# Moving store and load issues between the queues of a two-layer attention and spectral-convolution kernel: stores from SyncE to ScalarE two steps later, branch-matrix loads from SyncE to GpSimd

## The chip, the cores and the metric

The kernel runs on one core of one Trainium2 chip. A core has five engines with instruction streams of their own: TensorE (PE in the profile; its weight loads are shown apart as PEld), VectorE (DVE), ScalarE (ACT), GpSimd (POOL) and SyncE (SP). Any of ACT, SP and POOL can issue a DMA here; the profile shows the issuing part of an engine with a trailing q (SPq, ACTq, POOLq). The metric is the device time in microseconds (us) of one execution, and the median over the runs is compared.

## The reference

The input `x` has the shape (2, 128, 64, 64): two images, 128 channels, 64 x 64 positions. There are two layers.

```python
# layer 0, on x transposed to (2, 64, 64, 128)
x = LN(neighbourhood_attention_7x7(LN(x)) ) @ w1.T + x      # 4 heads of 32
x = LN(relu(LN(x) @ w2.T)) @ w3.T + x
# layer 1, on the tokens t of each image, (2, 4096, 128)
q   = LN(t)
sim = q @ q.T / sqrt(128);  sim[diagonal] = -1e9
t   = t + softmax(sim) @ q
u   = LN(t)
t   = t + sum over the 4 branches of  w[branch] * stu(u[: fraction], branch)
# stu: 16 causal filters phi of the sequence's length, by FFT,
#      once on u and once on u with alternating signs,
#      each filter's output through M_phi_plus[branch, k] or M_phi_minus[branch, k],
#      scaled by sigma[k] ** 0.25, summed over k; plus a three-tap filter M_u[branch]
```

The four branches use the whole sequence, a half, a quarter and an eighth of it, and their weights come from a hard Gumbel softmax over four numbers. The kernel combines the four branches' matrices with these weights first (per segment of the sequence), and so applies one set of matrices.

## The kernel before

**Stages.** By time in the profiled execution: layer 0 until about 345 us; the self-attention of image 0 from about 345 to 830 us; that of image 1 from 830 to 1242 us; leftover pieces of the work filled in until about 1300 us, called the end in what follows; and the spectral convolution from 1300 us on, which is a long row of small PE products (`burst` and `project`, L1565 and L1584) with copies out of PSUM by DVE and ACT. The convolution in the frequency domain reads its input from two arrays in DRAM: `us`, the transformed tokens, and `gs`, the transformed filters.

**The attention, `attention(b, fill)`.** The 4096 tokens of an image are 8 chunks of 512. As the similarity matrix is symmetric, only the 36 pairs (a, c) of chunks with a <= c are computed. Each pair takes four steps. For a pair, PE makes the similarities in a PSUM bank (`bank`, L927 or L936), ACT takes their exponential into `e` (L932 or L943), one pair ahead of its use. PE then multiplies `e` with the tokens for the rows of chunk c (`other`, L1057). The same weights are needed transposed for the rows of chunk a (`own`, L985). Pairs with a = c need no transposed half: there PE uses `es[j]` at once (L949 transposes the part under the diagonal, and the diagonal's products are also recorded at L985). For all "far" pairs (a != c, and not the last neighbours 6 and 7) the transposition goes over DRAM:

- `sent` (L959): ACT issues the write `eb<-e`, 1 MB, after the pair's fourth exp. There are four `eb` buffers in DRAM and two `e` buffers.
- `moved` (L966), two steps (MOVE) later: SP issues four reads `et<-eb` of 256 KB that put the blocks of 32 rows in their transposed place. There are two `et` buffers.
- `turned` (L975), seven steps (TURN) after the write: DVE transposes within blocks of 32 x 32.
- `pair_onto`/`onto` (L985), from eight steps (DELAY) after the write on: PE's `own` products.

Within the attention, from some 430 us on, the program order of PE, DVE, ACT, POOL and SP is the order in which the Python code issues the instructions (a manual schedule); before that, only the marked instructions keep it. So an instruction that waits holds all later ones of its engine.

**The work filled in, `fill()`.** At each step the attention calls `fill()`. It first calls `stores()`, which issues all DMA writes that the earlier steps appended to the list `behind_`, and then advances one generator by one step:

```python
        def stores():
            while behind_:
                to, src = behind_.pop(0)
                nc.sync.dma_start(out=to, in_=src)
```

The generators that matter here:

- `after(b, c)` finishes chunk c of image b, 16 chunks in all. It divides by the softmax's sum (L1105 transposes `xa` in a bank), adds the residual, normalises to `z` (the line L174 `ln_rs`, on POOL, is its power), and then makes a forward transform in three groups of products (`tr` and `z`, L1156 and L1169). For each group, ACT copies the banks to `uo` (L1138, two buffers), the `adder` (POOL) makes sums and differences `ub` (L1141, four buffers), and DMA writes `us<-ub` are appended (L1145 and L1148): 4, 4 and 8 of them for the three groups, so 16 for a chunk and 256 in all.
- `branch_weights` loads four matrices `m_u` (`st<-in_m_u`), combined on DVE with the branches' weights `wt`.
- `filters` loads the filters (`pn`) on SP, transforms them (L1360) and makes `fb` and `fn` on POOL (L1372, L1383; they share the four `ub` buffers); 32 DMA writes `gs<-fb` and `gs<-fn` are appended (L1347).
- `for_ffn` calls `filter_matrices`, which loads 32 blocks of `m_plus` and `m_minus` (`st`, two buffers in each of two pools), three ahead of their use, and combines them on DVE to `mpl` and `mmi` (L1299 and L1301). Then SP loads `inv` (L1499) and the first blocks `ct` and `ut` of the convolution (L1459 and L1467).
- `short_lags` makes the three-tap filter: it writes `xa` back by transposes and ACT copies, and multiplies with `mu` (lag products).

All branch loads (`m_u`, `m_plus`, `m_minus`) go through `branch()` (L1274 to L1278):

```python
            st = (pool or sp).tile([P, 4, P], F32, tag="st", name="st")[:, 0 : src.shape[1]]
            nc.sync.dma_start(out=st, in_=src[i].rearrange("k d e -> d k e"))
```

**The end.** After the second attention `adder` becomes DVE, and the generators that are left, two chunks and their `short_lags`, are advanced in turn with a `stores()` after each step. Then come the residual's lag products (`residuals`) and the convolution, whose input is read on SP (`ct` and `ut`) as long as it runs.

Of the kernel before, what the change touches and what calls it, by code (L numbers as in the profile page):

```python
# [14 lines left out]
P = 128  # L15
# [87 lines left out]
def kernel(  # L103
# [16 lines left out]
    nc = tc.nc  # L120
# [14 lines left out]
    for c in range(4):  # L135
# [23 lines left out]
        out=flip, in_=flip, compare_op=ALU.not_equal, fill=1.0, base=1 - QT * QT, pattern=[[0, 2], [1, QT * QT]],  # L159
# [16 lines left out]
    def ln_statistics(src):  # L176

        n = src.shape[1]
        st = lnp.tile([P, 4, 6], F32, tag="ln_st", name="ln_st")
        mv = lnp.tile([P, 4, 2], F32, tag="ln_mv", name="ln_mv")  # L180
        rs = lnp.tile([P, 4], F32, tag="ln_rs", name="ln_rs")
        for j in range(n):
            nc.vector.bn_stats(st[:, j, :], src[:, j, :])
            nc.vector.bn_aggr(mv[:, j, :], st[:, j, :])
        rsqrt(rs[:, :n], mv[:, :n, 1], 1e-5)
        return mv, rs

    def ln_apply(dst, src, stats):
        mv, rs = stats
        for j in range(src.shape[1]):  # L190
            nc.vector.tensor_scalar(
                dst[:, j, :], src[:, j, :], mv[:, j, 0:1], rs[:, j : j + 1], ALU.subtract, ALU.mult
            )
# [5 lines left out]
    def transposed(ps, src):  # L199

        for j in range(src.shape[1]):
            nc.tensor.transpose(ps[:, j * P : (j + 1) * P], src[:, j, :], ident)  # L202
# [37 lines left out]
    with l0a:  # L240
# [34 lines left out]
        def table(ci, h, eng):  # L275
# [16 lines left out]
            out=gavg, in_=gavg, compare_op=ALU.is_ge, fill=0.0, base=0,  # L292
# [3 lines left out]
            out=gavg, in_=gavg, compare_op=ALU.is_ge, fill=0.0, base=3,  # L296
# [11 lines left out]
        for h in range(HEADS):  # L308
            src = bass.AP(rpb.tensor, rpb.offset + h * RPR * RPW + 50, [[RPW, QT], [1, QT], [1, RLEN]])
# [567 lines left out]
    with ap_:  # L877
# [6 lines left out]
        def bank():  # L884
            return ps_m.tile([P, 512], F32, tag="bank", name="bank")
# [5 lines left out]
            out=tr.rearrange("p h e c -> p (h e) c"),  # L891
            in_=nc.inline_tensor(t_in, "t_in").ap().rearrange("(h p) c -> p h c", p=P),
# [195 lines left out]
        adder = [nc.gpsimd]  # L1088
        behind_ = []

        def stores():
            while behind_:
                to, src = behind_.pop(0)
                nc.sync.dma_start(out=to, in_=src)


        def after(b, c):

            yield True
            n0 = 4 * c  # L1100
            par, hf = divmod(c, 4)
            hh, fp = divmod(hf, NFP)
            pt = bank()
            for j in range(4):
                nc.tensor.transpose(pt[:, j * P : (j + 1) * P], xa[b][:, (n0 + j) * P : (n0 + j + 1) * P], ident)  # L1105
            rden = sp.tile([P, 4], F32, tag="rden", name="rden")
            kept_, out_ = tt[b][:, n0 : n0 + 4, :], pt.rearrange("p (j d) -> p j d", d=P)
            nc.vector.reciprocal(rden, out_[:, :, P - 1])
            rest = sp.tile([P, 4], F32, tag="rest", name="rest")
            nc.vector.tensor_reduce(rest, out_[:, :, 0 : P - 1], AX.X, ALU.add)  # L1110
            for j in range(4):
                nc.vector.scalar_tensor_tensor(
                    kept_[:, j, 0 : P - 1], out_[:, j, 0 : P - 1], rden[:, j : j + 1], kept_[:, j, 0 : P - 1],
                    ALU.mult, ALU.add,
                )
            nc.vector.tensor_tensor(rest, rest, rden, ALU.mult)
            nc.vector.tensor_tensor(kept_[:, :, P - 1], kept_[:, :, P - 1], rest, ALU.subtract)
            yield
            borrowed = b == 1 and spare not in ([], [None])
            z = spare.pop() if borrowed else sp.tile([P, 4, P], F32, tag="z4", name="z4")  # L1120
            stats = ln_statistics(kept_)
            yield True
            yield True
            ln_apply(z, kept_, stats)
            yield
            yield True
            pt = bank()
            transposed(pt, z)
            s0 = 1 + 2 * P * hh * FB
            to = zc[b][:, par, s0 : s0 + 2 * P * FB].rearrange("p (c e f) -> p e f c", e=2, f=FB)  # L1130
            nc.scalar.copy(to[:, :, 2 * fp : 2 * fp + 2], pt.rearrange("p (e f c) -> p e f c", e=2, f=2))
            yield

            def store(pu, n, r0, m, ri):

                for s in range(2):
                    both = sp.tile([P, 512], F32, tag="uo", name="uo", bufs=2)
                    nc.scalar.copy(both[:, 0 : 2 * n], pu[s][:, 0 : 2 * n])  # L1138
                    ub = sp.tile([P, 2, 256], F32, tag="ub", name="ub", bufs=4)
                    for sgn, op in enumerate((ALU.add, ALU.subtract)):  # L1140
                        adder[0].tensor_tensor(ub[:, sgn, 0:n], both[:, 0:n], both[:, n : 2 * n], op)  # L1141
                    for sgn in range(2):
                        to = us[r0 : r0 + m, sgn, :, 2 * hh + s, 2 * fp : 2 * fp + 2, b, par, :]
                        if ri is not None:
                            behind_.append((to[:, ri], ub[:, sgn, :].rearrange("p (f d) -> p f d", d=P)))  # L1145
                            continue
                        for f in range(2):
                            behind_.append((to[:, :, f].rearrange("k i d -> i k d"), ub[64 * f : 64 * f + 64, sgn, 0:P]))  # L1148

            for r0, c0 in row_tiles:  # L1150
                for ri in range(2):
                    pu = [bank() for _ in range(2)]
                    for e in range(2):
                        for s in range(2):
                            rows_ = slice(s * 64, (s + 1) * 64)
                            nc.tensor.matmul(  # L1156
                                pu[s][:, e * 256 : (e + 1) * 256], lhsT=tr[rows_, hh, e, c0 + ri * P : c0 + (ri + 1) * P],
                                rhs=z[rows_, 2 * e : 2 * e + 2, :].rearrange("p f d -> p (f d)"), start=True, stop=True,
                            )
                    store(pu, 256, r0, P, ri)  # L1160
                    if FB == 4 or ri:
                        yield

            pu = [bank() for _ in range(2)]
            for e in range(2):
                for f in range(2):
                    for s in range(2):
                        rows_ = slice(s * 64, (s + 1) * 64)
                        nc.tensor.matmul(  # L1169
                            pu[s][f * 64 : (f + 1) * 64, e * P : (e + 1) * P], lhsT=tr[rows_, hh, e, left_col:],  # L1170
                            rhs=z[rows_, 2 * e + f, :], start=True, stop=True,
                        )
            store(pu, P, left_row, 32, None)
            yield

            if borrowed:
                spare.append(None)
# [96 lines left out]
        def branch(src, i, pool=None):  # L1274

            st = (pool or sp).tile([P, 4, P], F32, tag="st", name="st")[:, 0 : src.shape[1]]
            nc.sync.dma_start(out=st, in_=src[i].rearrange("k d e -> d k e"))
            return st.rearrange("p k e -> p (k e)")  # L1278

        def filter_matrices(mpl, mmi, pool):  # L1280
# [36 lines left out]
        def filters():  # L1317
# [24 lines left out]
            def store(src, r0, n, ri, s, i, o):  # L1342
                to = bass.AP(
                    gs.tensor, gs.offset + r0 * 4 * SG * GROW + (i * SG + s) * GROW + o * LL,
                    [[4 * SG * GROW, n], [2 * SG * GROW, 2], [1, LL]],
                )
                behind_.append((to, src))  # L1347

            everything = [(r0, c0 + ri * P, (ri,), P) for r0, c0 in row_tiles for ri in range(2)]
            everything.append((left_row, left_col, (0, 1), 64))  # L1350
            for r0, c0, parts_, m in everything:
                places = cm[1][:, SG * LL : (3 * SG) * LL].rearrange("p (j e c) -> p j e c", j=SG, e=2)
                for j in range(SG):
# [21 lines left out]
                    for at, ri in enumerate(parts_):  # L1375
                        mine = slice(at * n, (at + 1) * n)
                        store(fb[mine], r0, n, ri, s, 0, ri)
                        if ri == 0:
                            store(fb[mine], r0, n, ri, s, 1, 1)
# [136 lines left out]
        while chains:  # L1516
            for gen in chains[:2]:
                if next(gen, 0) == 0:
                    chains.remove(gen)
                stores()  # L1520
            next(kept[0], None)
        for _ in residuals:
            next(kept[0], None)
        for _ in kept[0]:
# [11 lines left out]
    with ExitStack() as cv:  # L1536
# [133 lines left out]
        def place_of(o, par, a):  # L1670
            return o[:, :, a % 2, a // 2, :, par].rearrange("p c f -> p f c")
# [68 lines left out]
        for h in range(2):  # L1740
# [12 lines left out]
            for par in range(2):  # L1753
                for a in range(4):
                    to = place_of(o, par, a)
# [100 lines left out]
```

## Time and profile before

| | |
|---|---|
| median of 3 runs | 2059.06 us (2057.91 to 2060.68) |
| the profiled execution | 2061.56 us, its span 2059.8 us |
| mean granted clock of TensorE | 0.971 |
| SP's hardware queue (q1) | 162.59 MB, 32.1% of the time of 16 DMA engines |
| ACT's hardware queue (q10) | 58.04 MB, 7.0% |
| POOL's software queue (q0) | 576 packets, 2.10 MB, 0.3% |
| writes `eb<-e`, on ACT | 54 of 1024 KB |
| reads `et<-eb`, on SP | 216 of 256 KB |

The span is the time from the first to the last instruction of the profiled execution; the metric has some 1.8 us around it. A row of the profile names a line of the kernel, the engine, and the operation as out<-in with shapes. A wait is written as waiter <- releaser, and its time is idle time of the waiting engine just before an instruction. In the waits of a queue (SPq) the wait of the issuing engine before a DMA goes out is meant. Idle time of an engine that is not the bottleneck costs nothing by itself.

### The profile page before, as it was taken

The numbers are of one execution on the slowest core, as the hardware profiler recorded it, in microseconds if no ns is written. First come the engines' busy times: TensorE is split into PE (matmuls) and PEld (weight loads), VectorE is DVE, ScalarE is ACT, GpSimd is POOL, SyncE is SP. The second block draws the span as 40 slices with busy tenths as digits, with TensorE's granted clock in tenths as the row PEclk, the third lists the DMA queues.
The fourth block names the chain that finished last, engine by engine and source line by source line (L and its number), as shares of the span: only waits on it lengthen the run. The fifth ranks groups of instructions, "written<-read, shape, count | busy, mean of one in ns | idle before, by whom it ended". The sixth has DMA issues, their size and how long they took to land.

```text
span 2059.8 us, 50961 instructions
## 1 busy us (share of the span) xinstructions
PE 1924.6 (93%) x20504; PEld 1355.8 (66%) x20504; DVE 941.0 (46%) x2918; ACT 733.1 (36%) x1718; POOL 570.6 (28%) x954
## 2 busy tenths in 40 slices
PE   6899998999899999897978898999999999999998
PEld 4677775444444444443433344799999899999987
DVE  5799995443544343242533336333333334333332
ACT  3789885312223323222312232222222222222222
POOL 4467986303422113101101111022222121222211
PEclk8999999999999999999989999999999999999999
DMA  5222221667656534648865632222222123222211
GB/s 153 62 62 62 62 58 31 191 149 232 188 154 178 159 108 150 172 119 209 226 173 160 182 112 73 70 68 67 66 67 60 51 56 103 68 66 67 67 45 43
DMA packets 278378, 225.97 MB, mean 110 GB/s; under 512 B 122607, under 2 KB 241535, under 8 KB 270720
## 3 DMA queue, kind: packets, MB, share of 16 engines
q1 hardware_dynamic: 269442, 162.59, 32.1%
q10 hardware_dynamic: 8126, 58.04, 7.0%
q8 instruction: 163, 2.67, 0.5%
q0 software_dynamic: 576, 2.10, 0.3%
q14 instruction: 71, 0.58, 0.1%
HBM read 131.40 MB, written 91.25 MB: 108 GB/s over the span
## 4 chain that ended last, share of the span: by engine, by line
PE 75%; DVE 8%; DMA 5%; POOL 4%; issue 4%; ACT 1%; SPq 1%; DVEq 0%; POOLq 0%; ACTq 0%
PE acc L1584 27%; PE own L985 10%; PE bank L927 7%; PE pc L1565 7%; PE other L1057 6%; PE bank L349 2%; PE bank L559 2%; PE bank L202 2%; PE bank L1156 2%; DMA et<-eb 2%; PE bank L1199 1%; DMA eb<-e 1%; DVE et L975 1%; PE bank L523 1%; PE po L581 1%
## 5 line engine op out<-in xcount | busy, mean ns | idle before, releaser
L1570 DVE COPY y<-pc 128x512 f32<-128x512 f32 x320 | 206.1, 686 | 347.4 <-PE pc L1565 345.9
L1584 PE MATMUL acc<-y,mpl 32*128 32x256 f32 x5120 | 324.9, 380 | 0.8 <-DVE af L1594 0.8
L1584 PE MATMUL acc<-y,mmi 32*128 32x256 f32 x5120 | 316.5, 375 | 0.0
L1570 ACT COPY y<-pc 128x512 f32<-128x512 f32 x320 | 171.9, 589 | 392.7 <-PE pc L1565 379.1
L1584 PEld LDWEIGHTS acc<-y,mpl 32*128 32x128 f32 x5120 | 289.9, 186 | 8.3 <-DVE af L1594 1.3
L1584 PEld LDWEIGHTS acc<-y,mmi 32*128 32x128 f32 x5120 | 290.9, 185 | 3.9
L985 PE MATMUL own<-et,tok 128*128 128x512 f32 x448 | 225.9, 629 | 61.2 <-DVE et L975 49.1
L932 ACT ACTIVATE e<-bank 128x512 f32<-128x512 f32 x216 | 128.8, 599 | 308.0 <-PE bank L927 302.7
L1057 PE MATMUL other<-e,tok 128*128 128x512 f32 x448 | 230.9, 597 | 6.5 <-DVE xa L1066 6.5
L927 PE MATMUL bank<-cm 128*128 128x512 f32 x432 | 227.3, 608 | 0.0
L1565 PE MATMUL pc<-ct,ut 32*128 32x256 f32 x2560 | 212.5, 377 | 3.1 <-DVE y L1570 3.1
L1595 POOL TENSOR_TENSOR af<-af 128x512 f32<-128x512 f32 x39 | 49.7, 1275 | 589.2 <-DVE af L1594 589.2
L985 PEld LDWEIGHTS own<-et,tok 128*128 128x128 f32 x448 | 86.9, 199 | 177.5 <-issue 108.7
L1565 PEld LDWEIGHTS pc<-ct,ut 32*128 32x128 f32 x2560 | 172.7, 186 | 9.3 <-DVE y L1570 5.2
L975 DVE STREAM_TRANSPOSE et<-et 128x1024 f32<-128x1024 f32 x108 | 127.7, 1221 | 67.6 <-DMA et<-eb 66.3
L174 POOL TENSOR_TENSOR ln_rs<-ln_rs,mhalf 128x4 f32<-128x4 f32 x24 | 25.3, 1054 | 480.6 <-DVE ln_rs L173 480.5
L1057 PEld LDWEIGHTS other<-e,tok 128*128 128x128 f32 x448 | 81.6, 191 | 100.0 <-issue 84.0
L1141 POOL TENSOR_TENSOR ub<-uo 128x256 f32<-128x256 f32 (+1 forms) x160 | 96.5, 640 | 178.1 <-ACT uo L1138 167.5
L927 PEld LDWEIGHTS bank<-cm 128*128 128x128 f32 x432 | 76.9, 194 | 73.5 <-issue 67.8
L546 ACT ACTIVATE p<-p,mn 128x196 f32<-128x196 f32 x256 | 114.4, 449 | 14.4 <-DVE mn L536 13.8
L1138 ACT COPY uo<-bank 128x512 f32<-128x512 f32 (+1 forms) x96 | 46.9, 517 | 125.3 <-PE bank L1156 96.6
L943 ACT ACTIVATE e<-bank 128x512 f32<-128x512 f32 (+1 forms) x72 | 32.6, 455 | 139.0 <-DVE bank L941 133.9
(261 smaller groups left out, 2559.7 us busy)
## 6 DMA issues: line engine op xcount, KB each, us to landing
eb<-e ACTq DMA_DIRECT2D x54, 1024.0 KB
et<-eb SPq DMA_DIRECT2D x216, 256.0 KB
ut<-us SPq DMA_DIRECT2D x160, 128.0 KB
us<-ub SPq DMA_DIRECT2D x128, 128.0 KB
ct<-gs SPq DMA_DIRECT2D x320, 40.0 KB
vw<-vd SPq DMA_DIRECT2D x256, 49.0 KB
ct<-gs SPq DMA_DIRECT2D x320, 32.0 KB
vd<-v SPq DMA_DIRECT2D x128, 32.0 KB
```

The source lines that it names most:

```text
L546: nc.scalar.activation(p, p, AF.Exp, bias=t[name + "mn"][:, h : h + 1], scale=-1.0, accum_out=t["den"][:, u, h : h + 1],)
L927: nc.tensor.matmul(ps.rearrange("p (q t j) -> p q t j", q=4, t=4), lhsT=cm[b][:, n * P : (n + 1) * P], rhs=keys.rearrange("p (t q j) -> p ...
L932: nc.scalar.activation(e, ps.rearrange("p (q r) -> p q r", q=4), AF.Exp, bias=0.0, scale=ASCALE)
L975: in_place(nc.vector.transpose(flat, flat))
L985: nc.tensor.matmul(out_, lhsT=tok[b][:, n, :], rhs=e, start=first, stop=last, skip_group_check=True)
L1057: nc.tensor.matmul(turn(other, "p (q r) -> p q r"), lhsT=tok[b][:, n, :], rhs=es[j], start=(j == 0), stop=(j == 3),)
L1138: nc.scalar.copy(both[:, 0 : 2 * n], pu[s][:, 0 : 2 * n])
L1141: adder[0].tensor_tensor(ub[:, sgn, 0:n], both[:, 0:n], both[:, n : 2 * n], op)
L1565: nc.tensor.matmul(pcs[j].rearrange("p (g o c) -> p o g c", g=4, o=2)[:, :, at], lhsT=ut[rows_, par, :], rhs=cv_[rows_], start=True, stop= ...
L1570: (nc.scalar.copy if j % 2 else nc.vector.tensor_copy)(y[:, :, :, 4 * kl + j, :], pcs[j].rearrange("p (g x k) -> p k g x", g=4, k=KF))
L1584: nc.tensor.matmul(acc[j][:, 0:256], lhsT=(mmi if l else mpl)[rows_, k, :], rhs=y[rows_, k, 2 * l : 2 * l + 2].rearrange("p s n x -> p (s ...
L1595: eng.tensor_tensor(af[:, 0:2], af[:, 0:2], af[:, 2:4], ALU.add)
```

## The change

Three things change. `stores()` issues its DMA writes on ACT. It takes a second list: the sums append to `fresh_`, and what is in `fresh_` moves to `behind_` at the end of a call, so that a write goes out at the second call of `stores()` after its sums were issued. `branch()` issues its loads on POOL. As the last writes would now be left in the two lists, two more calls of `stores()` stand after the leftover generators. SP keeps the reads `et<-eb`, the loads of `pn` and `inv`, and the blocks `ct` and `ut`.

```diff
@@ attention and fill @@
         behind_ = []
 
+        fresh_ = []
+
         def stores():
-            while behind_:
-                to, src = behind_.pop(0)
-                nc.sync.dma_start(out=to, in_=src)
+            for to, src in behind_:
+                nc.scalar.dma_start(out=to, in_=src)
+            behind_[:] = fresh_
+            fresh_.clear()
@@ store() in after(): the us writes @@
                         if ri is not None:
-                            behind_.append((to[:, ri], ub[:, sgn, :].rearrange("p (f d) -> p f d", d=P)))
+                            fresh_.append((to[:, ri], ub[:, sgn, :].rearrange("p (f d) -> p f d", d=P)))
                             continue
                         for f in range(2):
-                            behind_.append((to[:, :, f].rearrange("k i d -> i k d"), ub[64 * f : 64 * f + 64, sgn, 0:P]))
+                            fresh_.append((to[:, :, f].rearrange("k i d -> i k d"), ub[64 * f : 64 * f + 64, sgn, 0:P]))
@@ branch() @@
             st = (pool or sp).tile([P, 4, P], F32, tag="st", name="st")[:, 0 : src.shape[1]]
-            nc.sync.dma_start(out=st, in_=src[i].rearrange("k d e -> d k e"))
+            nc.gpsimd.dma_start(out=st, in_=src[i].rearrange("k d e -> d k e"))
             return st.rearrange("p k e -> p (k e)")
@@ store() in filters(): the gs writes @@
-                behind_.append((to, src))
+                fresh_.append((to, src))
@@ the end @@
                 stores()
             next(kept[0], None)
+        for _ in range(2):
+            stores()
         for _ in residuals:
             next(kept[0], None)
```

## The prediction

> **What bounds the kernel now.** I read the page's busy table first: TensorE (PE) is at work 93% of the span, no other engine over half.
>
> ```profile
> PE 1924.6 (93%) x20504; PEld 1355.8 (66%) x20504; DVE 941.0 (46%) x2918; ACT 733.1 (36%) x1718; POOL 570.6 (28%) x954
> ```
>
> So a change of queues can win only where PE is idle, and PE's idle time by stage says where: 860.0 - 773.6 = 86 us in 440 to 1300 us (both attentions and the work filled between them), 760 - 745.4 = 15 us in the 760 us after it. The change acts in that first stage alone. Next, the waits of PE and of SyncE (SP) there (total, times, longest):
>
> ```profile
> PE own L985 <- DVE et L975: 49.1, 10, 12.4
> PE own L985 <- DMA ct<-gs: 7.2, 1, 7.2
> SPq L966 <- DMA eb<-e: 274.0, 28, 22.1
> SPq L1094 <- POOL ub L1141: 164.8, 91, 23.6
> SPq L1094 <- DMA eb<-e: 81.8, 14, 9.6
> ```
>
> PE waits for VectorE (DVE) to turn `et`. SP stands behind stores (L1094): 165 us for GpSimd's (POOL) sums, which is plain, and 82 us for `eb<-e`, which a store neither reads nor writes. The reason shows in the trace's semaphore waits: the DMAs of SP and ScalarE (ACT) take eight completion counters in turn, and one is issued only when the DMA eight before it has landed. The timelines of SP, DVE and PE at the largest gap (start, duration, in brackets the idle time before):
>
> ```profile
> 1024.15 20.16 SPq L1094 DMA_DIRECT2D us<-ub  x12
> 1044.37 1.65 SPq L1277 DMA_DIRECT2D st<-in_m_minus_dram  x3
> 1046.12 1.88 SPq L966 DMA_DIRECT2D et<-eb  x4
> ...
> 1048.31 0.49 DVE L1299 TENSOR_SCALAR mmi<-st,wt 128x512 f32<-128x512 f32 x1 [17.74 <-DMA st<-in_m_minus_dram]
> 1048.71 2.37 DVE L975 STREAM_TRANSPOSE et<-et 128x1024 f32<-128x1024 f32 x2
> ...
> 965.52 1.88 PE L985 MATMUL own<-et,tok 128*128 128x512 f32 x4
> ...
> 1051.13 3.78 PE L985 MATMUL own<-et,tok 128*128 128x512 f32 x4 [12.44 <-DVE et L975]
> ```
>
> Twelve stores hold SP for 20 us (two of their counters are those of `eb` writes, landed at 1033.7 and 1042.4); the branch load behind them comes late, DVE waits 17.7 us for it with the turn queued behind, and PE stops for 12.4 us. After the gap four products take 3.8 us where they take 1.9 undisturbed: a stop costs some 2 us more than itself.
>
> [...] DMA is busy 58% in this stage.
>
> **The change, part by part.**
>
> *a. 288 stores leave SP* (256 `us<-ub`, 32 `gs`). SP keeps the `et` reads and also the loads of `pn`, `inv`, `ct` and `ut`. PE gaps before `own` whose chain runs through SP held by stores or by loads behind them: 3.6 us (at 472), 3.6 (605), 6.9 (829: 15 stores from 799.7 to 818.6 ahead of the reads), 11.5 (961), 12.4 (1051), 7.2 (1147: reads behind 16 `ct` loads, these behind stores) = 45.2 us, and 6 restarts x 2 = 12. The stop of 6.9 us at 1102 stays: it hangs on the load of `inv`, which keeps its place. The same reads then have ample time: a turn is due 7 steps after its read, some 20 us, against 4 to 7 us for a read to land.
>
> *b. Branch loads go to POOL.* Four `m_u` loads: the stop at 434 to 437 (2.6 + 0.9 us) goes, 3.5. The 32 others are in the gaps of (a). The nearest row for their cost is the load of `xa` on POOL: 0.54 us for 128 rows. A branch load has 512 rows of 512 bytes: 0.54 us if paid per DMA, 2.2 if per row; 32 of them 17 to 70 us, beside 17 us of other POOL work in 900 to 1070. POOL has room; a load may lag behind sums that now wait for a later store, and I take 2 us lost (0 to 10).
>
> *c. The stores go to ACT*, 256 x 0.48 + 32 x 0.59 = 142 us of issue at SP's medians; ACT's own DMAs (`eb<-e`) take 0.33, so 95 to 142. ACT is busy 233 of 860 us: the sum fits. What counts is what queues behind them: the exp that feeds PE's next products, the copies `uo` that free PSUM banks, and the `eb` writes. The delay of two steps hides the POOL wait. The counters do not go away: the eight stores of a chunk's last group stand just behind an `eb` write in most chunks of the built order, and the sixth to eighth wait until it has landed, 3.9 to 5.5 us after its issue. So ACT is held about 0.3 + 8 x 0.48 + 2.5 = 7 us there. PE has its exp made a pair, four steps, ahead and five banks; steps take 1.7 to 4.7 us, so a hold of 7 us is nearly covered. I take 0.5 us for each of 13 chunks, 6 us. Less covered: diagonal pairs, where PE needs each exp in the next step (L949): four behind a group at 1 us, two with stores between their exps at 3 us, 10 us in all; and the change of batch at 770 to 830, 3 us.
>
> *d. The `gs` stores* (497 to 551 us). POOL's sums wait for buffers that are now freed one step later; the chain landing (5) + sums (2.9) + issue takes some 9 us in two steps of 6.4, so ACT falls about 6 us behind. Against it POOL is no longer held by SP's `eb` waits, and gaps of 2.2 and 4.8 us there (528, 540) go. Net 0 (-5 to +8).
>
> *e. The end*, 1250 to 1300. 48 stores x 0.48 = 23 us are added to ACT's 16 in these 50 us, in line with the copies of `uo` and, now behind the last store, those of `xa` that PE's lag products need. I take 8 us lost (3 to 14).
>
> *f.* The new flush issues the last groups; its cost is in (e).
>
> **The sum**: -45.2 - 12 - 3.5 = -60.7; +2 + 6 + 10 + 3 + 0 + 8 = +29; net about -32. Of a sum with so many covers I keep -30. The profiled execution took 2061.56 us (span 2059.8 and 1.8 around it), 2.5 above the median 2059.06; taken off the median this gives 2029.
>
> **Rivals.**
>
> *R1, slower: ACT becomes the queue that stops PE.* Speaking for it: all 82 us of counter waits on `eb` and every POOL wait that two steps do not cover move into the stream that makes PE's input. Against: ACT is idle 73% of this stage. If a hold's uncovered part is 5 us (the landing of an `eb` write) in the 13 chunks, they cost 65 instead of 6, so +29: 2088; with 3.5 us, 2068. It decides from (60.7 - 23) / 13 = 2.9 us per chunk up.
>
> *R2, the loads stay late.* If the branch loads on POOL land as late as from SP (sums, store landing and 2.2 us of issue ahead of them; the `xa` loads took 6 to 8.7 us to land), the stops at 961 and 1051 stay: 24 + 4 us less gain, 2057. Against: POOL is free from 939 to 1005 in the trace.
>
> *R3, the covers hold.* Costs of (c) and (e) near 8 us in all: 2008. Against: the end is nearly full on ACT.
>
> *R4, it does not do what it says.* The built order shows the stores on ACT and the loads on POOL, so I give this nothing of its own; a balance by chance within 0.2% is R1 at 2.9 us per chunk or R2.
>
> **How the numbers follow.** Forecast 0.50, its own range 2012 to 2048. R1 0.27 (2060 to 2090; 0.03 of it within 0.2%). R2 0.12 (2050 to 2062; a third of it within 0.2%). R3 0.11. 0.2% is 4 us, about what a measurement of this kernel can tell from no change. Faster: 0.50 + 0.08 + 0.11 = 0.69, less 0.02 for a forecast's tail, 0.67; same 0.07; slower 0.26. For eight times in ten I leave out the upper part of R1 and the lower of R3: 2006 to 2076.
>
> **What would show it.** Right: SP's waits at the store line are gone; `own <- DVE et L975` falls from 49 to under 15 us; DVE's waits for `st` (18.2 and 17.7) go under 3; the ACT queue shows some 290 more issues and waits of 2 to 5 us at the store line, on `eb<-e`; PE's idle time in 440 to about 1270 us is near 55. Wrong: PE idle before `bank` or L949 products with ACT as the releaser, over 30 us in all, would be R1; DVE still waiting over 10 us for `st` would be R2; a stage from 1250 on longer by over 14 us would mean that (e) is mis-sized.

## The result, and the profile after

The changed kernel takes 2050.56 us (median of 7 runs, 2046.24 to 2054.53) where the kernel before takes 2059.06 in the same comparison: the ratio is 0.9954, 95% interval 0.9940 to 0.9968. That is 9.5 us faster (7 to 12). The forecast was 30 us faster, so the direction held and the size did not: about a third came.

The profiled execution took 2047.53 us (span 2045.8), 14.0 less than the one before. That is 5.5 more than the medians differ by: the traced run before lies 2.5 us above its median, this one 3.0 below it. The busy table has hardly moved, except that POOL now issues branch loads:

```profile
PE 1928.6 (94%) x20504; PEld 1361.0 (67%) x20504; DVE 942.2 (46%) x2918; ACT 728.9 (36%) x1718; POOL 598.2 (29%) x990
```

The waits tell more (waiter, releaser: total, times, longest). First those of PE and ACT, then those of SP's reads, and last one of PE in the trace before, for comparison:

```profile
PE own L985 <- DVE et L975: 23.6, 7, 7.1
PE bank L949 <- ACT e L943: 18.2, 10, 4.7
ACT e L932 <- DMA us<-ub: 31.9, 5, 13.9
ACT e L943 <- DMA us<-ub: 25.5, 4, 9.7
```

```profile
SPq L966 <- DMA eb<-e: 513.9, 50, 53.8
SPq L966 <- DMA us<-ub: 88.9, 34, 6.7
```

```profile
PE bank L949 <- ACT e L943: 7.0, 5, 2.6
```

PE's wait for the turned `et` has halved (49.1 before), and its 7.2 us behind `ct` are gone. Against that, PE waits 18.2 us for exponentials, where it waited 7.0 before. ACT stands idle for up to 13.9 us in front of one. SP has lost its waits at the store line, 165 and 82 us, but its reads still wait 89 us for `us<-ub`, stores that SP no longer issues. SP also waits 514 us for `eb<-e`, up from 274: with the stores gone it often comes to its reads before the data is there.

**Where the time went.** Stretches between the starts of ACT's exponentials (L932 and L943, counted through both images) can be compared directly. The third column is what the prediction's items (a), (b: `m_u`) and (e) give for the stretch; its 19 us of holds on ACT and 2 for POOL are not assigned to one.

| stretch, us in the trace before | before | after | difference | predicted |
|---|---|---|---|---|
| layer 0, to the first exp, 0 to 348 | 347.7 | 349.7 | +2.0 | 0 |
| exp 0 to 40, to 453 (`m_u`) | 104.9 | 100.3 | -4.6 | -3.5 |
| exp 40 to 48, to 478 (stop at 472) | 25.5 | 25.4 | -0.1 | -5.6 |
| exp 48 to 112, to 680 (`gs`, stop at 605) | 202.1 | 203.9 | +1.8 | -5.6 |
| exp 112 to 160, to 815 | 134.4 | 135.5 | +1.1 | 0 |
| exp 160 to 192, to 930 (stop at 829) | 115.2 | 106.7 | -8.5 | -8.9 |
| exp 192 to 240, to 1092 (961 and 1051) | 162.7 | 149.3 | -13.4 | -27.9 |
| exp 240 to 287, to 1240 (1147) | 147.7 | 143.5 | -4.2 | -9.2 |
| the end, to the first `y` copy, 1292 | 52.3 | 61.3 | +9.0 | +8 |
| convolution | 767.5 | 770.3 | +2.8 | 0 |

Over all 14 traces of this study layer 0 takes 345.6 to 350.5 us and the convolution 766.2 to 772.2 without any edit there, so 2 or 3 us in these two rows mean nothing. Without these two rows the trace after is 18.9 us ahead, twice the 9.5 us of the medians. The stretches are from one execution each, so part of this gain is chance, and the table cannot say in which row.

### The profile page after: what moved, and what is told of

It reads as the page before. It is cut to its first block, busy times and chain, and to the rows that moved or that the text cites. A ratio compares the mean times of both kernels' runs of the same rounds, so it can differ in the third digit from the quotient of the medians.

```text
span 2045.8 us, 50912 instructions
## 1 busy us (share of the span) xinstructions
PE 1928.6 (94%) x20504; PEld 1361.0 (67%) x20504; DVE 942.2 (46%) x2918; ACT 728.9 (36%) x1718; POOL 598.2 (29%) x990
## 3 DMA queue, kind: packets, MB, share of 16 engines
q1 hardware_dynamic: 202050, 127.18, 25.5%
q10 hardware_dynamic: 57022, 84.26, 11.5%
## 5 line engine op out<-in xcount | busy, mean ns | idle before, releaser
L985 PE MATMUL own<-et,tok 128*128 128x512 f32 x448 | 221.3, 618 | 28.7 <-DVE et L975 23.6
L932 ACT ACTIVATE e<-bank 128x512 f32<-128x512 f32 x216 | 127.7, 600 | 283.2 <-PE bank L927 229.4
L975 DVE STREAM_TRANSPOSE et<-et 128x1024 f32<-128x1024 f32 x108 | 127.7, 1220 | 75.9 <-DMA et<-eb 67.9
L174 POOL TENSOR_TENSOR ln_rs<-ln_rs,mhalf 128x4 f32<-128x4 f32 x24 | 25.4, 1056 | 346.4 <-DVE ln_rs L173 346.4
L943 ACT ACTIVATE e<-bank 128x512 f32<-128x512 f32 (+1 forms) x72 | 32.4, 456 | 132.6 <-DVE bank L941 91.8
```

The costliest lines, as they stand in the source:

```text
L932: nc.scalar.activation(e, ps.rearrange("p (q r) -> p q r", q=4), AF.Exp, bias=0.0, scale=ASCALE)
L975: in_place(nc.vector.transpose(flat, flat))
L985: nc.tensor.matmul(out_, lhsT=tok[b][:, n, :], rhs=e, start=first, stop=last, skip_group_check=True)
```

## The experiments

All medians are of device time; each ratio is to the kernel before, run beside it. "A" is the stretch from the first exponential to the first `y` copy of the convolution in the trace, which leaves the two rows of chance out. It is from one execution of each kernel; where it and the medians differ, the medians count.

| kernel | median us | ratio (95% interval) | A, us |
|---|---|---|---|
| before | 2059.06 | 1 | 944.7 |
| changed | 2050.56 | 0.9954 (0.9940 to 0.9968) | 925.8 |
| 1 branch loads alone | 2050.37 | 0.9959 (0.9944 to 0.9973) | 931.9 |
| 2 stores alone | 2051.64 | 0.9961 (0.9949 to 0.9973) | 936.0 |
| 3 stores on SP, two steps | 2054.16 | 0.9978 (0.9970 to 0.9986) | 930.8 |
| 4 stores on ACT, one step | 2045.70 | 0.9937 (0.9922 to 0.9952) | 925.1 |
| 5 all stores on POOL | 2078.41 | 1.0090 (1.0073 to 1.0107) | 956.8 |
| 6 end's stores on SP | 2043.12 | 0.9917 (0.9900 to 0.9934) | 919.6 |
| 7 four stores a step | 2036.25 | 0.9883 (0.9859 to 0.9906) | 917.9 |
| 8 `inv` multiplied later | 2036.78 | 0.9887 (0.9871 to 0.9904) | 917.8 |
| 9 `us` on POOL, loads on SP | 2048.79 | 0.9942 (0.9920 to 0.9963) | 930.4 |
| 10 turn and `own` a step later | 2085.66 | 1.0119 (1.0102 to 1.0136) | 967.3 |
| 11 combination | 2024.38 | 0.9824 (0.9807 to 0.9840) | 900.9 |
| 12 combination, `pn` unhindered | 2020.76 | 0.9826 (0.9805 to 0.9847) | 897.7 |

### 1 to 3: the parts

**1, branch loads alone** (kernel before, with the load in `branch()` on POOL):

```diff
-            nc.sync.dma_start(out=st, in_=src[i].rearrange("k d e -> d k e"))
+            nc.gpsimd.dma_start(out=st, in_=src[i].rearrange("k d e -> d k e"))
```

> Only the branch loads move to POOL; the stores stay on SP, one step behind their sums. Theory A (the stop at DVE comes from the branch loads that stand behind the stores, and the stores on ACT are about a wash): the stops at 434, 961 and 1051 us go, 3.5 + 11.5 + 12.4 us less what is late next, so 2035 to 2045 us, as fast as the whole change or faster. Theory B (the stores held SP and so the et reads; the loads were only caught in it): the reads stay late behind the stores, the stops before own stay at over 30 us in 440 to 1300 us, 2052 to 2058 us.

2050.37 us, between the two ranges. The `m_u` stop is gone; the stops at 961 and 1051 shrink from 11.5 and 12.4 us to 9.3 and 5.5; those at 469, 602, 827, 1091 and 1135 stay (3.7, 3.8, 7.5, 7.1, 7.5). (Those of 9.3 and 5.5 us stand a pair later than those of 11.5 and 12.4.) So theory B is right that the reads stay late, and A is right that half of the 1051 stop was the branch load itself.

**2, stores alone** (changed kernel, with the load in `branch()` back on SP).

> Only the stores move (to ACT, two steps behind); the branch loads stay on SP. Theory A: 2055 to 2062 us, since the holds of ACT and the longer end (9 us) eat what the reads gain, and DVE keeps some wait for st. Theory B: 2050 to 2054 us, nearly all of the change's gain, with the wait own <- DVE et L975 near the 24 us of the whole change.

2051.64 us, and the wait of `own` is near the 24 us that theory B named. The end takes 62.4 us, much as in the changed kernel (61.3).

**3, stores on SP two steps behind:**

```diff
             for to, src in behind_:
-                nc.scalar.dma_start(out=to, in_=src)
+                nc.sync.dma_start(out=to, in_=src)
```

> As the changed kernel, but the stores go out on SP, two steps behind their sums. ACT is free of them. Theory A: the POOL sums are always ready, the end costs 9 us less than in the change, the ACT holds go: 2035 to 2043 us. Theory B: SP still waits for the counters of eb writes ahead of the et reads (82 us before), so stops before own of over 30 us stay: 2050 to 2057 us.

2054.16 us, with stops before `own` of 9.1, 8.7, 7.1 and 9.8 us left: theory B. The two steps alone do not free SP. At the store line it still waits 77 us for POOL's sums and 66 for `eb` writes, where it was 165 and 82.

In the medians each part alone gives nearly what both give: 8 and 8 us against 9.5, each within some 3 us. In the traces the two parts' gains in A are 12.8 and 8.7 us, and 18.9 together, which would be nearly additive. How far the two parts overlap is not shown.

### 4: one step

```diff
-            for to, src in behind_:
-                nc.scalar.dma_start(out=to, in_=src)
-            behind_[:] = fresh_
+            behind_.extend(fresh_)
             fresh_.clear()
+            while behind_:
+                to, src = behind_.pop(0)
+                nc.scalar.dma_start(out=to, in_=src)
```

> As the changed kernel, but the stores go out on ACT one step behind their sums, as they did on SP. If the second step is what hides POOL's sums from ACT: ACT waits for POOL ub in most of the 48 groups, 1 to 2 us each, 2056 to 2075 us and PE stops before bank products or L949. If the counters set the hold anyway: within 4 us of the changed kernel, 2047 to 2054 us.

2045.70 us, a little under the second range, and A is 925.1 against 925.8. The second step is not what keeps ACT going: without it ACT waits for POOL in a few places (longest 5.5 us), but its longest hold at stores falls from 13.4 to 7.1 us, and no group of eight stores stands directly behind an `eb` write in ACT's order any more, where seven of the thirteen in the attentions do in the changed kernel. On this evidence it is no slower, perhaps a little faster.

### 5 and 9: are shared completion counters what still holds the reads?

The stop at 958 us in the changed kernel, in the timelines of SP, DVE and PE (start, duration, in brackets the idle time before):

```profile
937.64 10.70 SPq L966 DMA_DIRECT2D et<-eb  x4
...
955.39 2.37 DVE L975 STREAM_TRANSPOSE et<-et 128x1024 f32<-128x1024 f32 x2 [9.50 <-DMA et<-eb]
...
957.82 3.78 PE L985 MATMUL own<-et,tok 128*128 128x512 f32 x4 [5.57 <-DVE et L975]
```

Nothing stands between the four reads in SP's order, yet they take 10.7 us to issue. Three of them, at 943.94, 946.01 and 948.04 us, start 0.01 to 0.02 us after a `us<-ub` of ACT has landed. In the profiler's trace of the changed kernel each DMA is listed with the semaphore that counts its landing: all 1769 of SP and ACT have one of the same eight (100 and 102 to 108), the 40 of POOL one of eight others (111 to 118). For 1593 of the 1769 the trace lists a wait for the same semaphore before they go out, and 1410 take the one that was used eight DMAs before. These three reads wait for 102, 104 and 105, which ACT's stores of 932.8, 935.6 and 936.5 us had taken before them.

**5, all stores on POOL** (the store line with `nc.gpsimd`).

> As the changed kernel, but the stores are issued on POOL (two steps behind), whose DMAs have counters of their own. Theory C (what is left of the stops comes from the eight counters that SP and ACT share: a read waits until an unrelated store has landed): SP's waits on us<-ub (89 us) go, the stop of 5.6 us at 958 falls under 2, the L949 stops at 523 to 528, 655 and 1107 us (4.9 + 3.5 + 4.7 us) go, the end shortens by some 5 us: 2030 to 2040 us. Rival D (whatever engine issues 288 stores is held by them): POOL's issue of 0.75 us each, 216 us, delays ln_rs and the sums, PE stops before bank L202 and own grow by over 15 us: 2055 us or more.

2078.41 us: the total is rival D's, the mechanism of C is half seen. SP's waits on `us<-ub` are gone, and so are the stops at 655 and 1107. But POOL's own stream is now the one that stops PE, by 19.9 us at 560 alone. POOL's timeline before it:

```profile
551.53 1.40 POOL L1375 TENSOR_TENSOR fb<-cm 64x256 f32<-64x256 f32 x2 [1.06 <-DMA gs<-fb]
553.01 1.49 POOL L1386 TENSOR_SCALAR fn<-fb 32x512 f32<-32x512 f32 x1
554.56 1.62 POOL L1095 DMA_DIRECT2D gs<-fb  x3
556.10 0.62 POOL L1095 DMA_DIRECT2D gs<-fn  x1
556.59 1.72 POOL L1095 DMA_DIRECT2D gs<-fb  x3
558.08 0.76 POOL L1095 DMA_DIRECT2D gs<-fn  x1
558.91 1.05 POOL L174 TENSOR_TENSOR ln_rs<-ln_rs,mhalf 128x4 f32<-128x4 f32 x1
```

`ln_rs`, which PE's transposes hang on, stands behind all stores and sums of the filters. The stop at 982 (7.4 us) hangs on a branch load queued behind stores on POOL, so this run could not tell what makes the one at 958.

**9, `us` on POOL, `gs` on ACT, branch loads on SP:**

```diff
-                nc.scalar.dma_start(out=to, in_=src)
+                (nc.scalar if to.tensor is gs.tensor else nc.gpsimd).dma_start(out=to, in_=src)
...
-            nc.gpsimd.dma_start(out=st, in_=src[i].rearrange("k d e -> d k e"))
+            nc.sync.dma_start(out=st, in_=src[i].rearrange("k d e -> d k e"))
```

> As the changed kernel, but the us stores are issued on POOL, the gs stores stay on ACT, and the branch loads go back to SP, where no store stands before them. The stop of 5.6 us at 958 in the changed kernel: if it comes from completion counters that the reads share with ACT's stores (the reads wait 7 us on us<-ub), it falls under 2 us here, and so does the one of 2.9 at 1041, and the time from exp 192 to exp 240 falls from 149.4 to 141 to 144 us. If it comes from the trip over DRAM being too slow in itself, both stay within 1.5 us. In total the POOL issues cost as in the run with all stores there (late ln_rs): 2045 to 2070 us.

The timelines of SP and PE at the same place:

```profile
948.88 1.75 SPq L966 DMA_DIRECT2D et<-eb  x4
...
965.54 1.98 PE L985 MATMUL own<-et,tok 128*128 128x512 f32 x4 [2.01 <-DVE et L975]
```

The four reads go out in 1.75 us, SP has no wait on `us<-ub` left, the stop is 2.0 us, that of `own` at 1041 is gone (one of 1.9 us before L949 stands at 1048), and exp 192 to 240 takes 143.0 us, in the range of the counter theory. With that, most of the stop at 958 is shown to hang on the counters: the reads share them with ACT's stores. What is left of it hangs on a branch load, which is on SP again in this run, and so does a new stop of 3.8 us at 977: DVE waits 6.5 us for `st`, with the diagonal's mask (L941) queued behind. The total (2048.79) pays for that and for late `ln_rs` at 591 and 666 us (3.4 and 6.1).

### 6: the end

`store_queue` is a list that holds ACT's queue until then:

```diff
-                nc.scalar.dma_start(out=to, in_=src)
+                store_queue[0].dma_start(out=to, in_=src)
...
         adder[:] = [nc.vector]
+        store_queue[:] = [nc.sync]
```

> As the changed kernel, but from the end of the second attention on the stores go out on SP. The time from the last exp to the first y copy was 52.3 us before, 61.3 in the changed kernel: it falls back to 52 to 54 us, and the total by 7 to 9, to 2041 to 2044 us. If the extra time in the end is only work shifted from before it (the traces of the change are ahead by 26 us there), the stretch stays near 60 us and the total at 2050.

2043.12 us, the end 51.8 us instead of 61.3. So the extra time in the end came from the stores on ACT. This kernel is the changed one up to the end, and its trace is there 2.8 us behind that of the change: a measure of chance for one trace.

### 7: four stores a step

```diff
-            for to, src in behind_:
+            for to, src in behind_[:4]:
                 nc.scalar.dma_start(out=to, in_=src)
-            behind_[:] = fresh_
+            behind_[:] = behind_[4:] + fresh_
```

At the end `stores()` is called until both lists are empty, instead of twice.

> As the changed kernel, but at most four stores are issued in one step. If the number of issues in line (8 x 0.5 us) makes the holds of ACT: the L949 stops at 655 and 1107 us fall from 3.5 and 4.7 to under 2 us each, and the total by 3 to 6, 2045 to 2047 us. If the wait for the counter of the eb write just ahead makes them: the stops stay within 1.5 us, and the total within 3 us of the changed kernel, or the stores that come later hold the reads on SP longer, 2051 to 2055 us.

2036.25 us, a larger gain than either theory had. The stops at 655 and 1107 fall nearly as the first one said, but only a part of the 14 us is theirs. The hold that it breaks up, in the changed kernel (ACT, then PE):

```profile
650.54 0.34 ACTq L959 DMA_DIRECT2D eb<-e  x1
650.98 7.28 ACTq L1095 DMA_DIRECT2D us<-ub  x8
658.30 0.98 ACT L943 ACTIVATE e<-bank 128x512 f32<-128x512 f32 x2 [7.79 <-DMA us<-ub]
...
658.95 0.48 PE L949 MATMUL bank<-ident,e 128*128 128x128 f32 x1 [3.52 <-ACT e L943]
```

With four a step, this stop is 1.1 us and the one at 1107 falls from 4.7 to 2.1. The longest hold of ACT falls from 13.4 to 8.5 us, at the same total (189 and 190 us from 440 to 1240). So what costs here is the length of one hold, not the sum of all. From the first to the last exponential the trace is 8.8 us shorter.

### 8: what one stop is worth

```diff
+            for _ in range(4):
+                yield
             for s, (lo, hi) in enumerate(((0, CQ // 8), (CQ // 8, CQ // 4), (CQ // 4, CQ // 2), (CQ // 2, CQ))):
                 nc.vector.tensor_scalar(inv[:, :, lo:hi], inv[:, :, lo:hi], seg[:, s : s + 1], None, ALU.mult)
```

> As the changed kernel, but DVE's four multiplications of inv come four fill steps after its load (before: in the same step, with the turn of et queued behind them). This takes one stop of known length (7.1 us at 1081) away and measures what a stop is worth. If a stop costs 2 us more than its length, as the prediction added: the time from exp 240 to exp 287 falls by 9 us; if it costs its length: by 7 us; if something else is late right behind it, by less than 4 us.

2036.78 us. Exp 240 to 287 takes 133.5 us instead of 143.5: 10 us less, of which 7.1 are the stop and 0.8 a shorter one at 1107; 2 us remain. The busy time by windows of the changed kernel shows them (after the busy times come PEclk, DMA share and GB/s): the stop, the 4 us behind it, and the next 4; then the stop of 3.5 us at 659 and the 4 us behind it.

```profile
1073.80:1080.90 7.10, 0.01 (x1) 0.00 (x0) 3.30 (x7) 0.00 (x0) 0.00 (x0) 0.77 0.77 228
1080.90:1085.00 4.10, 4.09 (x8) 1.55 (x10) 2.81 (x3) 0.00 (x0) 0.00 (x0) 0.56 0.02 4
1085.00:1089.00 4.00, 4.00 (x16) 1.75 (x12) 0.00 (x0) 1.66 (x3) 2.52 (x4) 1.00 0.00 0
655.40:658.90 3.50, 0.04 (x1) 0.00 (x0) 0.30 (x1) 0.60 (x2) 0.00 (x0) 0.85 0.48 125
658.95:662.95 4.00, 4.00 (x11) 2.57 (x12) 0.29 (x1) 0.92 (x2) 0.10 (x1) 0.50 0.93 203
```

PE's granted clock is 0.56 in the 4 us after the stop of 7.1 us and 1.00 in the next 4; after the stop of 3.5 us it is 0.50, and 0.78 in the next 4 (662.95 to 666.95). By these means, as an estimate, 1.8 us are lost behind the first and 2.9 behind the second: of these two the shorter stop lost more.

### 10: a longer way for `et`

```diff
-MOVE, TURN, DELAY = 2, 7, 8
+MOVE, TURN, DELAY = 2, 8, 9
```

> As the changed kernel, but the turn of et comes 8 and the own products 9 steps after the write of eb (before: 7 and 8). If the stops that stay at 469 and 588 us (3.5 and 2.9 us) hang on the landing of the eb write and not on SP being held, one step of 1.7 us or more takes at least half of each away and leaves them under 2 us, the stop at 958 shrinks by 2 to 3 us, and with the slow clock after each stop the total falls by 6 to 12 us: 2039 to 2045 us. If they hang on a queue, they stay, and et is held longer: 2049 to 2056 us.

2085.66 us; neither case was right. The stops at 469 and 588 did shrink to 1.8 us each, but stops of `own` of about 2 us, 31 in all, stand all over the attentions now (waits of PE, then of SP):

```profile
PE own L985 <- DVE et L975: 67.7, 31, 7.6
```

```profile
SPq L966 <- PE own L985: 84.3, 20, 10.4
```

There are two `et` buffers, and a later `own` gives them back later: the reads wait 84 us for that (26 in the changed kernel over the same time). That this makes the new stops is likely, but not shown. So the run did not settle the stop at 469.

### 11 and 12: a faster version, and the stop at 469

**11** puts four edits into the changed kernel: stores one step behind, at most four a step, on SP in the end, and `inv` multiplied four steps later.

> The changed kernel with four edits together: stores one step behind their sums, at most four in one step, on SP from the end of the second attention on, and the multiplication of inv four steps after its load. If the parts lie in different places, the differences of the traces add: -2 -9 -10 -9, so near 2021 us; if one step and four a step take away the same stops: 2024 to 2030 us; if they add as their medians did (-5 -14 -14 -7): 2011 us.

2024.38 us, in the range where one step and four a step share their gains. The longest hold of ACT is 6.7 us.

**12** adds the one edit:

```diff
-                pn = sp.tile([P, KF, 2, LG], F32, tag="st", name="pn")
+                at_ = (3 * SG + 2 * hh + e) * LL
+                pn = cm[1][:, at_ : at_ + LL].rearrange("p (k l f) -> p k l f", k=KF, l=2)
```

> The combination with one edit more: the four loads of pn go to columns of cm[1] that are free then, not to the two st buffers, so that they don't wait on SP until DVE has copied the two before (8 us in the changed kernel), with the et reads behind them. If the stop at 469 us, which no placing of the stores and branch loads has moved (3.4 to 3.8 us in nearly all runs), hangs on that wait, it goes with the slow clock after it: exp 40 to exp 56 shortens by 4 to 6 us, and the total is 2018 to 2021 us. If it hangs on the trip of eb over DRAM, it stays within 1 us, and the total is 2022 to 2026.

SP's and PE's timelines in run 11, and then in run 12, at the same products:

```profile
442.92 11.05 SPq L1327 DMA_DIRECT2D pn<-in_phi_pad_dram  x3
454.07 13.28 SPq L966 DMA_DIRECT2D et<-eb  x8
...
463.72 1.02 PE L1057 MATMUL other<-e,tok 128*128 128x512 f32 x2
468.32 3.68 PE L985 MATMUL own<-et,tok 128*128 128x512 f32 x4 [3.58 <-DVE et L975]
```

```profile
436.39 12.46 SPq L1328 DMA_DIRECT2D cm<-in_phi_pad_dram  x3
452.14 12.58 SPq L966 DMA_DIRECT2D et<-eb  x8
...
465.81 1.02 PE L1057 MATMUL other<-e,tok 128*128 128x512 f32 x2
466.67 1.88 PE L985 MATMUL own<-et,tok 128*128 128x512 f32 x4
```

The stop is gone, and exp 40 to 56 shrinks from 55.2 to 49.4 us: 5.8 for a stop of 3.6. It hung on the loads of `pn`, which stood on SP ahead of the reads, waiting for DVE's copies out of their buffers (8.1 us in one piece in run 11, nothing in run 12). The total did not show it: 2020.76 against 2024.38, but the same ratio to the kernel before. In the trace A is only 3.2 us shorter: 1.2 us are lost before exp 40 and 2.7 from exp 56 to 112, which may be chance.

## Why the prediction was right or wrong

**Item (a), the gain of 57 us, is the step that failed.** It said that with the stores gone the reads "have ample time", and gave six stops and their restarts as gone. In the trace 16 of the 45 us of stops still stand: two stops went whole (829 and 1147), that at 472 stayed, that at 605 shrank to 1.0 us while one of 2.9 came ahead of it, and in place of those at 961 and 1051 two shorter ones stand a pair later.

The time of the reads was counted too long. The seven steps to a turn run from the write of `eb`, and the reads go out two steps after it, so five steps are left, not seven. At the stop of 958 us the "some 20 us" lie between the write (issued at 931.4) and PE's readiness for the products (952.2). The write takes 6.2 us of them to land. That leaves the reads 14.6 us, and the issue of the four takes 10.7. What used the time up differs from stop to stop:

- *The stop at 472 was read wrongly.* "SP held by stores or by loads behind them": it was held by the loads of `pn`, which wait for DVE's copies and which the change leaves on SP. No placing of stores moved it; run 12 did. 5.6 us.
- *In front of the stop at 605 a new one came at 588, by way of ACT.* The old one, now at 602, is 1.0 us. Before the new one ACT stands 7.6 us behind eight stores, its copy `tt` comes late, DVE's statistics wait for that copy and the turn of `et` is queued behind them; PE stops 2.9 us. In the lines that follow (ACT, DVE and PE of the changed kernel) the hold can be followed across three engines. The prediction considered only PE waiting for ACT itself. With one step instead of two (run 4) there is no stop of 2 us or more at either place.

```profile
574.76 7.56 ACTq L1095 DMA_DIRECT2D us<-ub  x8
582.36 0.59 ACT L232 COPY cm<-bank 128x512 f32<-128x512 f32 x1 [8.07 <-DMA us<-ub]
...
583.96 0.29 DVE L183 BATCH_NORM_STATS2 ln_st<-tt 128x6 f32<-128x128 f32 x1 [9.01 <-ACT tt L224]
...
588.29 2.53 PE L985 MATMUL own<-et,tok 128*128 128x512 f32 x4 [2.89 <-DVE et L975]
```

- *The stops at 961 and 1051 shrank from 23.9 to 8.5 us, not to nothing.* The prediction had read from the trace that SP and ACT take the eight counters in turn, and applied it to ACT's stores only. The trace after shows the other direction too: reads on SP wait for the landing of stores on ACT (88.9 us in all, 34 times). Moving the stores from SP to ACT did not take them out of the counters that SP's reads use. Run 9 shows it for the stop at 958; for the one at 1041 the same cause is likely, as it went in that run too.

**The restarts, -12 us in the sum, gained nothing on balance.** Two us for a stop was about the right price (run 8: 2 us beside the stops; 1.8 and 2.9 by the clock), but the number of stops of 2.8 us and more is nine before and nine after, since new ones came. The new stops were priced without it. By the clock record of the two traces PE worked at a granted clock of 0.5 for 52.1 us from 440 us to the convolution before, and for 52.2 us after: 8 us less in the attentions, 8 more in the end.

**Luck hid nearly half of that.** In the trace the sum reads, in the prediction's own items: -29 instead of -45 for the stops of (a), 0 instead of -12 for the restarts, -5 for the `m_u` stops, +8 instead of +21 for the costs on ACT and POOL, -2 for (d), +9 for (e), together -19 instead of -32. The gain of (a) was 28 us short, and costs set 13 us too high made up for nearly half of it.

**Item (c), 19 us of holds on ACT.** The mechanism was right, with its place: the group of eight behind an `eb` write. The size was off. The hold was put at 7 us in each of 13 chunks; it came in seven, with 7.3 to 13.4 us (the other six took 4.5 to 5.6). PE covered even the 13.3 us hold at 1015, where its exponentials lay a pair ahead, so the half microsecond for each was about right. But the diagonal pairs were put at 1 us, and two at 3: the stops before L949 at 655 and 1107 measured 3.5 and 4.7, and the granted clock was 0.50 in the 4 us behind each, which is 2 more. The stops are the 8 us in the sum above. That is R1's mechanism in the uncovered places only; R1 itself, 2.9 us and more per chunk, did not come.

**Item (d), the `gs` stores at 0**, was about right: the stops at 528 and 540 (7.0 us) went as it said, and two at 523 and 528 (4.9 us) came, on exponentials behind `gs` stores. What spoiled that stretch are the two items above: with the stops at 588 and 602 (3.9) for that at 605 (3.6), and the one at 655 (3.5), its stops are 12.3 us after and 10.6 before, which is its +1.8.

**Items (b) and (e) held.** The `m_u` stops went (-4.6 against -3.5); a branch load costs POOL 0.75 us to issue, between the two bounds, and DVE's longest wait for `st` is 6.2 us where it was 18.2 (R2's mechanism did not come, though "under 3" was too low; that the time lies in R2's range, 2050 to 2062, is chance). The end lost 9.0 us against 8, and run 6 gives them back.

**The signs named beforehand**: `own <- DVE et L975` is 23.6, not under 15; ACT's holds are up to 13.4 us, not 2 to 5; PE is idle 843 - 774.2 = 69 us from 440 us to 1283, where it was 86 and 55 were named. SP's waits at the store line went, as named, and no sign of being wrong came up: PE waits 25 us for ACT in all (18.2 of them at L949), not over 30, and the end is 9 us longer, not over 14.

The expected gain was there to be had, by other edits: with ACT's holds broken up, the end left on SP and `inv` out of the way, run 11 is 36 us (33 to 40) faster than the kernel before.

## What to carry to other kernels

Moving an issue to another engine can move its waits: here PE's at L949 for ACT's exponentials went from 7.0 to 18.2 us. SP and ACT draw their completion counters from one set of eight in this kernel's traces, and SP kept 88.9 us of waits for stores that it no longer issues: look for reads whose releaser is a transfer that they have nothing to do with. Before counting a stop as cured, name the one instruction in front of the late one on its engine; a queue with several kinds of work in it (here stores, `pn`, branch loads) can have a different culprit at each stop. Count the time between two steps of a chain from the step that really starts it. Issue moved work in small pieces (here ACT's longest hold fell from 13.4 to 8.5 us with four stores a step, and the time from 2050.56 to 2036.25), and price every stop that comes with the same restart as those that go (here 1.8 and 2.9 us behind two stops).

## What the runs showed of the hardware that was not expected

- In windows of 4 us right after a stop of PE (2 us at 523, where the next stop follows) the granted clock is 0.50 to 0.66 in the changed kernel, after nine of eleven stops of 2.4 to 7.1 us; after one of 2.4 us (at 523) and one of 3.2 us in the end (at 1267) it is 1.00. The clock record that the profiler took in this trace, behind these means, holds 1.0 and 0.5 alone, and its changes lie 3.41 us or a multiple of that apart. From 345 to 1300 us, in stretches of 3.41 us counted from its first entry and set beside PE's busy time in the same trace, it changes from 1.0 to 0.5 ten times. In the stretch ahead of each of these PE was busy for 0 to 40%; in the 250 stretches at 1.0 with 1.0 behind them it was busy for 45% or more. Ahead of all ten changes back to 1.0 PE was busy throughout a stretch (one such stretch, at 1248, has 0.5 behind it). The stops at 523 and 1267 fell across two stretches; PE was busy for 48% and 45% of those with the larger part. In this trace, then, the place of a stop counted beside its length. That is a count from one execution; why the clock changes is not shown. The mean granted clock is 0.971 before, 0.975 after and 0.982 in run 11.
- The issue of a `us` store takes 0.48 us on SP (kernel before) and 0.50 on ACT (changed kernel; both medians) and 0.70 on POOL (mean, run 5): 256 of them are 178.5 us of POOL's time. POOL's stores of 128 KB land in 2.3 us there (median).
